# Graph convolution, layer 1: own rows added by VectorE, last two blocks gathered as plain rows, team pairs moved forward

## The chip, the cores and the metric

The kernel runs on one core of a Trainium2 chip. The metric is the device time of one execution in microseconds (us). The median of three runs of the kernel before is 2106.76 us, the lowest 2104.33, the highest 2110.44. Five engines run their own instruction streams in order, each waiting for the others by semaphores: TensorE (PE; its weight loads are listed as PEld), VectorE (DVE), ScalarE (ACT), GpSimd (POOL) and SyncE (SP), which issues most transfers. GpSimd issues the indirect transfers (gathers).

## The reference

Three graph convolution layers on 6250 nodes with 100,000 edges and one self loop for each node, widths 256, 512, 512, 256, then a residual and a layer norm:

```python
deg = jax.ops.segment_sum(jnp.ones_like(dst, dtype=x.dtype), dst, num_segments=n)
dinv = jnp.where(deg > 0, jax.lax.rsqrt(deg), 0.0)
norm_edge = dinv[src] * dinv[dst]
h = x
for W, b in ((W1, b1), (W2, b2), (W3, b3)):
    h = h @ W
    msg = h[src] * norm_edge[:, None]
    agg = jax.ops.segment_sum(msg, dst, num_segments=n)
    h = jax.nn.relu(agg + b)
x = _layernorm(x + h, axis=-1)
```

The edges come sorted by destination. A node's sum has the rows of its sources and, through the self loop, its own row.

## The kernel before

**Blocks and steps.** The nodes are 50 blocks of 125. Each layer (`layer`, with i = 0, 1, 2 for layers 1, 2, 3) forms the sums of a block in one of two ways. A *dense* block is the product of a matrix of edge counts with all rows of the table, 50 products (L1254); the counts are themselves made on the chip in layer 1 by `counts` (comparisons on VectorE, L784; products, L856) for 26 blocks and kept in DRAM. A *gathered* block fetches the rows of its edges, 16 gathers of 128 rows each (L1165), and multiplies each by a one-hot matrix (L1117, L1192). One step of the loop in `layer` (the variable `chunk`) issues one gather, the product of a gather some steps back (the *lag*), a few dense products, and one step of each piece of work under way (`go`, `go_fixed`). Where 10 blocks begin, one more gather fetches the rest of their edges. Layer 1 gathers blocks 22 to 49: 28 x 16 + 3 = 451 steps. Layer 2 gathers blocks 12 to 49, layer 3 blocks 29 to 49.

**Two halves.** TensorE multiplies in a rounded format. To keep precision a row is held as two halves, the rounded value and what is left, side by side. In layer 1 from block 26 on (`BOTH_FROM`) the gather fetches rows that are split already (table `both`, 512 elements, 2 KB) into one of 11 buffers named `halves`. Below block 26 it fetches plain rows (256 elements, 1 KB) which are multiplied unsplit. In layers 2 and 3 plain rows are fetched into a ring in `room` and split on the chip: ScalarE casts (L1219) and VectorE subtracts (L1222). `SPLIT` holds for each layer the lags of the cast, the subtraction and the product; layer 1 has (0, 0, 5).

**Own rows.** `parts` holds the split rows of all nodes on the chip. In layers 1 and 3 a gathered block's sum begins with a product of the identity with the block's own `parts` (L1177), into the same PSUM bank as the gathered products.

**After a block of layer 1** (`after1`): ScalarE scales the second half of the sum by `dinv` (L1284), VectorE scales the first and adds it (L1286), TensorE transposes (L1275) and multiplies by W1 (L1301), VectorE adds the bias (L1306), ScalarE applies the relu (L1309), and SP stores the result into layer 2's table (L72). Layer 2's first gather waits for the whole of that table.

**Stores for comparisons.** `counts` writes its comparisons into a rotating set of stores in `room`, two at first; when gathers into plain rows end in layer 1 (block 26), a third (`late_hot_room`), which lies where part of the ring of plain rows was, is added.

**Teams.** Layer 2's first 12 blocks are dense, but computed by `teams`: four groups of three blocks, three banks, 50 rows of blocks to go over; one call of its `next` issues one *pair*, that is, the two products (L964) of a block's counts with both halves of a row block, and now and then the load of the next two row blocks (SP, L74, three buffers), casts of counts (ScalarE, L916) and the split of the next row block (L924 on ScalarE, L926 on VectorE). The teams begin in layer 1 as soon as its 22 dense blocks are done, at one pair a step, go on while layer 1's last blocks drain, and run on in layer 2 at one pair a step; a whole pass is 600 pairs. Near their end (`returning`) layer 2 gives back four split buffers that lie in `parts`.

**The step between the layers.** At step 1 of layer 2 ScalarE and VectorE begin to split gathered rows, in order, each waiting for its gather; whatever the teams want of them after that is behind it. At step 5 SP is given the loads of W2 and W3.

Of the kernel before, what the change touches and what calls it, by code (L numbers as in the profile page):

```python
# [26 lines left out]
Q = 125  # L27
# [22 lines left out]
FEW = 22  # L50
BOTH_FROM = 26
BOTH_LAG = 5
SPLIT = ((0, 0, BOTH_LAG), (1, 2, 8), (3, 4, 9))
EXTRA = 4
TEAM = 3
TEAMS = 4
# [338 lines left out]
def sorted_path(ctx: ExitStack, tc: tile.TileContext, x, edges, starts, found, wts, biases, room, late, out):  # L395
# [367 lines left out]
    def counts(blocks, places, rush=0, at_once=False):  # L763

        def bank_for_pair():
            if at_once:
                return common.popleft() if len(common) > SPARE and len(full) < COUNTING else None
            if held.get("tr", 0) == 0:
                held["tr"] = 1
                return tr_bank  # L770

        def bank_back(bank):
            if at_once:
                common.append(bank)
            else:
                cooling.append(ticks + SOON)

        def compared(out, numbers):
            shape = list(out.shape)
            nc.vector.tensor_tensor(out, near_cols[:, :shape[2]].unsqueeze(1).to_broadcast(shape),  # L784
                                    numbers.unsqueeze(2).to_broadcast(shape), op=ALU.is_equal)

        hot = {}
        total = len(blocks) * GB
        ticks = 0
        bank, pair, full, whole = None, [], [], []  # L790

        def oldest_copied():
            if full:
                copied(full[0][0])
                return True

        if at_once:
            early_copy[0] = oldest_copied

        cooling = []  # L800

        def copied(now_on):
            while cooling and cooling[0] <= now_on:
                cooling.pop(0)
                free("tr")
            while whole and whole[0][0] <= now_on:
                _, n = whole.pop(0)
                place = places[n % len(places)]
                own = place[:, blocks[n], :]
                nc.vector.tensor_tensor(own, own, loops[:Q, :Q], op=ALU.add)  # L810
                by_rows(nc.sync, place.rearrange("p k v -> p (k v)"), kept[blocks[n]], store=True)
                if at_once:
                    there.append(now + 1)
            while full and full[0][0] <= now_on:
                _, counted_in, ms = full.pop(0)
                n, u = divmod(ms[0], GB)
                place = places[n % len(places)]
                nc.scalar.copy(place[:, :, u * G:(u + len(ms)) * G].rearrange("p k (t r) -> p t k r", r=G),  # L818
                               counted_in.rearrange("p (t v) -> p t v", t=2)[:Q, :len(ms), :NB * G]
                               .rearrange("p t (k r) -> p t k r", r=G))  # L820
                bank_back(counted_in)
                if u + len(ms) == GB:
                    whole.append((now_on + 1, n))

        for s in range(total + 4):
            if s < total and s % GB == 0:
                while (blocks[s // GB] + 1) * GB > seen * Q:
                    yield 1
            if s < total and s % WIDE == 0:
                t, w = divmod(blocks[s // GB] * GB + s % GB, Q)  # L830
                hot_stores.rotate(-1)
                hot_lo = hot_stores[-1][:, :WIDE * Q].rearrange("p (w v) -> p w v", v=Q)
                hot_key = hot_stores[-1][:, WIDE * Q:].rearrange("p (w v) -> p w v", v=G * NB)
                hot[s // WIDE] = hot_lo, hot_key
                compared(hot_lo, slots[:, t, 0, w:w + WIDE])
                compared(hot_key[:, :3], slots[:, t, 1, w:w + 3])
            if s < total and s % WIDE == 2:
                t, w = divmod(blocks[s // GB] * GB + s % GB + 1, Q)
                compared(hot[s // WIDE][1][:, 3:], slots[:, t, 1, w:w + WIDE - 3])
            copied(ticks)  # L840
            m = s - 4
            if 0 <= m:
                while at_once and finished < FEW and m // GB >= finished + len(places):
                    ticks += 1
                    yield 1
                    copied(ticks)
                while bank is None:
                    bank = bank_for_pair()
                    if bank is None and at_once and full and full[0][0] <= ticks + COPIED - 2:
                        copied(full[0][0])  # L850
                    elif bank is None:
                        ticks += 1
                        yield 1
                        copied(ticks)
                hot_lo, hot_key = [h[:, m % WIDE] for h in hot[m // WIDE]]
                nc.tensor.matmul(bank[:Q, len(pair) * 256:][:, :G * NB], lhsT=hot_lo, rhs=hot_key,  # L856
                                 start=True, stop=True)
                pair.append(m)
                if len(pair) == 2 or m % GB == GB - 1:
                    full.append((ticks + (COPIED if at_once else ALONE_COPIED), bank, pair))  # L860
                    bank, pair = None, []
            if s % 2 if s < rush else s % 2 or not rush:
                ticks += 1
                yield 1
        while full or whole or cooling:
            ticks += 1
            yield 1
            copied(ticks)
# [166 lines left out]
    def layer(i, width, gathered, dense, after, rows, first=0, spacing=1.0, extras=(), filler=None):  # L1035
# [97 lines left out]
        def of_both(c):  # L1133

            n, b, _ = items[c]
            return i == 0 and (n * GRP if b is None else b) >= BOTH_FROM

        def halved(c):

            return 0 <= c < total and items[c][1] is not None and i > 0  # L1140
        acc = None

        of_ten, to_split = {}, {}
        ten_halves = split.popleft() if i == 1 else None
# [2 lines left out]
        def gather(c):  # L1147
            nonlocal turn
            n, b, j = items[c]
            table = both_halves if of_both(c) else tables[i]  # L1150
            if (i, b, j) == (0, BOTH_FROM, BOTH_LAG + 1):
                hot_stores.appendleft(late_hot_room)
            if b is None:
                row, at = split.popleft() if of_both(c) else shared[n % 2], rest[:, n, 0:1]
                of_ten[n] = row
                if i == 1:
                    to_split[c + SPLIT[i][2] + 1] = n
            elif of_both(c):
                row, at = split.popleft(), src[:, b, j:j + 1]
                split_rows[c] = row  # L1160
            else:
                row, at = rows[turn % len(rows)], src[:, b, j:j + 1]
                (landed if i > 0 else split_rows)[c] = row
                turn += 1
            nc.gpsimd.indirect_dma_start(out=row, out_offset=None, in_=table,  # L1165
                                         in_offset=bass.IndirectOffsetOnAxis(ap=at, axis=0))

        def product(c):
            nonlocal acc
            n, b, j = items[c]  # L1170
            if b is None:
                return
            if j == 0:
                acc = sum_bank("acc", 2 if i == 1 else 3)
                if i != 1:

                    nc.tensor.matmul(acc[:Q], lhsT=ident_r[:Q, :Q], rhs=parts[:, b], start=True, stop=False)  # L1177
            if i == 1 and j == KF - LATE:
# [4 lines left out]
            for k, row in several:  # L1183
# [5 lines left out]
                    hot = hot.bitcast(F32)  # L1189
                size = min(row.shape[1], HID)  # L1190
                for c0 in range(0, row.shape[1], size):
                    nc.tensor.matmul(acc[:Q, :size], lhsT=hot, rhs=row[:, c0:c0 + size], start=(i == 1 and k == c0 == 0),  # L1192
                                     stop=(k == KF and c0 + size == row.shape[1]))
            halves = several[0][1]
            if i == 1 and halves in loaned:
# [10 lines left out]
        with tc.manual_schedule():  # L1206
            more_hots()
            to_sum = 0
            for chunk in range(total + (SHORT if i == 1 else lag)):
                now = chunk  # L1210
                if i == 1:
                    lag = SPLIT[i][2] if returning is None else max(SHORT, SPLIT[i][2] - (chunk - returning) // 2)
                if chunk < total:
                    gather(chunk)
                if halved(chunk - hi_lag):
                    halves = split_rows[chunk - hi_lag] = split.popleft()
                    if i == 1 and halves in loaned:
# [13 lines left out]
                    to_sum += 1  # L1231
                go(chunk)
                go_fixed(chunk)
                until = min(len(dense) * NB, begun + int((chunk + 1 - first) * NB / spacing))
                if i == 0:
                    until = min(until, done + 3)
# [43 lines left out]
    def after1(b, acc, bank):  # L1280
        got = []
        yield from take("zs", 2)
        zs = work.tile([Q, HID], F32, name="szs")
        nc.scalar.activation(zs[:, :C], acc[:Q, C:], AF.Copy, scale=dinv[:, b:b + 1])  # L1284
        yield 1
        nc.vector.scalar_tensor_tensor(zs[:, :C], acc[:Q, :C], dinv[:, b:b + 1], zs[:, :C], op0=ALU.mult, op1=ALU.add)  # L1286
        common.append(acc)
        yield SOON + 2
        turns = yield from one_of_common(0)
# [388 lines left out]
```

## Time and profile before

| | |
|---|---|
| median of three runs | 2106.76 us |
| the profiled execution's own time | 2105.52 us |
| its span, first to last instruction | 2103.8 us |
| mean granted TensorE clock | 0.981 |
| busy share: TensorE, VectorE, ScalarE, GpSimd | 92%, 73%, 64%, 68% |
| HBM traffic over the span | 236 GB/s |
| layer 1's last gather, layer 2's first | 709.65 us, 726.91 us |
| layer 3's first gather | 1652.79 us |

A row of a group reads: line, engine, operation, output <- input, shapes, count | busy us, mean ns of one | idle us of the engine just before, and what ended it. A row of a timeline reads: start, duration, engine, line, operation, output <- input, shapes, count [idle us before <- what ended it]. A row of windows reads: stretch, its length, then for each engine the busy us and the number of instructions, the granted TensorE clock, the busy share of the DMA engines (a sum over packets, which can pass 1) and GB/s. A row of DMA issues ends with the median us from issue to landing. A matmul's duration is that of one in a pipeline; the next can start earlier.

### The profile page before, as it was taken

The numbers are of one execution on the slowest core, as the hardware profiler recorded it, in microseconds if no ns is written. First come the engines' busy times: TensorE is split into PE (matmuls) and PEld (weight loads), VectorE is DVE, ScalarE is ACT, GpSimd is POOL, SyncE is SP. The second block draws the span as 40 slices with busy tenths as digits, with TensorE's granted clock in tenths as the row PEclk, the third lists the DMA queues.
The fourth block names the chain that finished last, engine by engine and source line by source line (L and its number), as shares of the span: only waits on it lengthen the run. The fifth ranks groups of instructions, "written<-read, shape, count | busy, mean of one in ns | idle before, by whom it ended". The sixth has DMA issues, their size and how long they took to land.

```text
span 2103.8 us, 30100 instructions
## 1 busy us (share of the span) xinstructions
PE 1943.4 (92%) x8711; PEld 1513.4 (72%) x8711; DVE 1527.7 (73%) x2877; ACT 1338.6 (64%) x2552; POOL 1435.4 (68%) x1442
## 2 busy tenths in 40 slices
PE   3499999999998689999999999999989899999997
PEld 2377777777774457788878777778777787887775
DVE  5877677777776288877787677777887377777777
ACT  1566777677775367767777666677766466555553
POOL 2466766676667477766776677667776477777775
PEclk9999999999999899999999999999999999999998
DMA  7887989999999999999999999889997366767674
GB/s 166 257 254 220 251 238 245 241 263 249 245 263 323 271 276 264 262 276 276 264 265 259 263 268 270 252 228 287 276 262 227 98 185 182 191 175 191 178 187 120
DMA packets 238728, 497.92 MB, mean 237 GB/s; under 512 B 43633, under 2 KB 86215, under 8 KB 238553
## 3 DMA queue, kind: packets, MB, share of 16 engines
q0 software_dynamic: 125184, 315.61, 54.6%
q1 hardware_dynamic: 97529, 168.45, 29.3%
q10 hardware_dynamic: 15840, 11.86, 2.2%
q8 instruction: 70, 1.15, 0.2%
q14 instruction: 105, 0.86, 0.1%
HBM read 428.29 MB, written 67.46 MB: 236 GB/s over the span
## 4 chain that ended last, share of the span: by engine, by line
PE 64%; DMA 17%; issue 7%; POOL 4%; DVE 4%; ACT 3%; ACTq 1%; SPq 0%; DVEq 0%; POOLq 0%
PE sacc L1192 12%; DMA room<-tab,ssrc 11%; PE mat_ps L1254 6%; PE smm L1254 6%; PE win_ps L1254 6%; PE win_ps L1364 5%; PE sacc L1254 5%; POOL room L1165 4%; PE win_ps L1384 3%; DMA halves<-both,ssrc 3%; PE str L1254 2%; PE mat_ps L964 2%; PE smm L964 2%; PE sacc L964 2%; PE sacc L1301 2%
## 5 line engine op out<-in xcount | busy, mean ns | idle before, releaser
L1165 POOL DMA_INDIRECT room<-tab,ssrc x1008 | 1039.2, 1031 | 386.9 <-issue 162.5
L1222 DVE TENSOR_TENSOR halves<-room,halves 128x512 fp32r<-128x512 f32 (+1 forms) x733 | 404.2, 566 | 230.1 <-ACT halves L1219 224.7
L1219 ACT CAST halves<-room 128x512 fp32r<-128x512 f32 (+1 forms) x733 | 367.7, 521 | 240.1 <-DMA room<-tab,ssrc 176.6
L1192 PE MATMUL sacc<-halves,shot 128*125 128x512 f32 x1375 | 481.4, 411 | 23.2 <-DMA halves<-both,ssrc 14.0
L1165 POOL DMA_INDIRECT halves<-both,ssrc x384 | 363.0, 945 | 158.5 <-issue 37.0
L1126 ACT CAST piece<-room 125x625 fp32r<-125x625 uint8 x416 | 294.3, 716 | 74.7 <-DVE halves L1222 22.7
L1192 PEld LDWEIGHTS sacc<-halves,shot 128*125 128x125 f32 x1375 | 255.3, 189 | 100.9 <-DMA halves<-both,ssrc 23.3
L784 DVE TENSOR_TENSOR room<-near_cols,slots 128x625 bf16<-128x625 f32 (+2 forms) x390 | 294.3, 803 | 36.7 <-PE sacc L856 15.6
L1117 DVE TENSOR_TENSOR shot<-near_cols,sdlo 128x500 fp32r<-128x500 f32 x371 | 248.3, 669 | 15.7 <-PE smm L1192 6.3
L1364 PE MATMUL win_ps<-room,w_sb 128*128 128x250 f32 (+1 forms) x832 | 191.0, 372 | 12.4 <-ACT room L1338 6.3
L1254 PE MATMUL mat_ps<-parts,piece 125*125 125x512 f32 x650 | 188.2, 406 | 0.3 <-ACT piece L1126 0.3
L1364 PEld LDWEIGHTS win_ps<-room,w_sb 128*128 128x128 f32 x832 | 154.4, 192 | 40.1 <-ACT room L1338 8.4
L1222 DVE TENSOR_TENSOR parts<-room,parts 128x512 fp32r<-128x512 f32 x211 | 143.7, 692 | 46.7 <-ACT parts L1219 41.2
L1254 PE MATMUL win_ps<-parts,piece 125*125 125x512 f32 x600 | 172.0, 408 | 5.0 <-ACT piece L1126 5.0
L1254 PE MATMUL smm<-parts,piece 125*125 125x512 f32 x605 | 173.0, 404 | 0.8 <-DVE piece L1126 0.6
L1219 ACT CAST parts<-room 128x512 fp32r<-128x512 f32 x211 | 128.7, 622 | 62.9 <-DMA room<-tab,ssrc 39.4
L926 DVE TENSOR_TENSOR parts<-parts 125x512 fp32r<-125x512 f32 x200 | 138.1, 691 | 35.2 <-ACT parts L924 34.8
L964 PE MATMUL sacc<-parts 125*125 125x512 f32 x400 | 140.4, 427 | 23.2 <-ACT parts L924 17.3
L1254 PE MATMUL sacc<-parts,piece 125*125 125x512 f32 x450 | 142.3, 423 | 2.5 <-ACT piece L1126 2.5
L818 ACT CAST room<-sacc 125x500 uint8<-125x500 f32 (+1 forms) x152 | 105.6, 703 | 60.8 <-PE sacc L856 59.2
L856 PEld LDWEIGHTS <-room 128*125 128x125 bf16 x650 | 88.9, 139 | 74.0 <-issue 26.6
L964 PE MATMUL mat_ps<-parts 125*125 125x512 f32 x400 | 137.1, 424 | 0.7 <-DVE st L1306 0.7
(308 smaller groups left out, 3139.4 us busy)
## 6 DMA issues: line engine op xcount, KB each, us to landing
parts<-tab SPq DMA_DIRECT2D x106, 448.0 KB
kept<-room SPq DMA_DIRECT2D x29, 683.6 KB
room<-kept SPq DMA_DIRECT2D x29, 683.6 KB
room<-tab,ssrc POOLq DMA_INDIRECT x1008, 5.5
tab<-st SPq DMA_DIRECT2D x62, 224.0 KB
both<-parts SPq DMA_DIRECT2D x10, 1120.0 KB
own_row<-tab SPq DMA_DIRECT2D x38, 224.0 KB
parts<-kept SPq DMA_DIRECT2D x60, 136.7 KB
```

The costliest lines, as they stand in the source:

```text
L784: nc.vector.tensor_tensor(out, near_cols[:, :shape[2]].unsqueeze(1).to_broadcast(shape), numbers.unsqueeze(2).to_broadcast(shape), op=ALU. ...
L818: nc.scalar.copy(place[:, :, u * G:(u + len(ms)) * G].rearrange("p k (t r) -> p t k r", r=G), counted_in.rearrange("p (t v) -> p t v", t=2 ...
L926: nc.vector.tensor_sub(to[:, HID:], row, to[:, :HID].bitcast(F32))
L964: nc.tensor.matmul(team_banks[n][:Q], lhsT=team_pieces[(g * CUTS + k // PIECE) % 2][n][:, k % PIECE, :], rhs=both_parts[u % 3][:, h * HID: ...
L1117: nc.vector.tensor_tensor(hot[:, :n], near_cols[:, :Q].unsqueeze(1).to_broadcast([P, n, Q]), dlo.rearrange("p b j -> p (b j)")[:, at:at + ...
L1126: convert(piece, made_or_read[:, c * PIECE:(c + 1) * PIECE, :])
L1165: nc.gpsimd.indirect_dma_start(out=row, out_offset=None, in_=table, in_offset=bass.IndirectOffsetOnAxis(ap=at, axis=0))
L1192: nc.tensor.matmul(acc[:Q, :size], lhsT=hot, rhs=row[:, c0:c0 + size], start=(i == 1 and k == c0 == 0), stop=(k == KF and c0 + size == row ...
L1219: nc.scalar.copy(halves[:, :width], landed[chunk - hi_lag])
L1222: nc.vector.tensor_sub(halves[:, width:], landed.pop(chunk - lo_lag), halves[:, :width].bitcast(F32))
L1254: nc.tensor.matmul(acc_d[:Q], lhsT=got[done // PIECE][:, k % PIECE, :], rhs=parts[:, k], start=(k == 0), stop=(k == NB - 1))
L1364: nc.tensor.matmul(h_ps[:, f, :], lhsT=w2_sb[:, k, (f2 + f) * P:(f2 + f + 1) * P], rhs=zt2[:, k, :wide], start=(k == 0), stop=(k == KH - 1))
```

## The change

- Own rows, layer 1, blocks 26 to 49: the identity product is not issued, and the first gathered product starts the bank. In `after1` VectorE adds `parts` to the whole sum (512 wide), ScalarE scales the second half in SBUF, VectorE scales and adds the first.
- Blocks 48 and 49 of layer 1 (`TAIL_FROM`) are gathered as plain rows into the ring in `room` and split on the chip, with lags 3 and 4. The lag of the product is 7 over the steps of block 48 (`TAIL_LAG`) and 5 elsewhere. The ring needs the third store's place: `counts` drops that store from its 22nd block on.
- One more team pair is issued at odd steps of layer 1 from the first gather of block 48 to the loop's end, and 12 (`FRONT`) at step 1 of layer 2 ahead of its first split.

```diff
+TAIL_FROM = 48
+TAIL_LAG = 7
+FRONT = 12
-SPLIT = ((0, 0, BOTH_LAG), (1, 2, 8), (3, 4, 9))
+SPLIT = ((3, 4, BOTH_LAG), (1, 2, 8), (3, 4, 9))
...
                 hot_stores.rotate(-1)
+                if at_once and s >= FEW * GB and hot_stores[-1] is late_hot_room:
+                    hot_stores.pop()
+                    hot_stores.rotate(-1)
...
-            return i == 0 and (n * GRP if b is None else b) >= BOTH_FROM
+            return i == 0 and (n * GRP >= BOTH_FROM if b is None else BOTH_FROM <= b < TAIL_FROM)
...
-            return 0 <= c < total and items[c][1] is not None and i > 0
-        acc = None
+            return 0 <= c < total and items[c][1] is not None and (i > 0 or items[c][1] >= TAIL_FROM)
+        acc = own_product = None
...
-                (landed if i > 0 else split_rows)[c] = row
+                assert i > 0 or b < TAIL_FROM or len(hot_stores) == 2
+                (landed if halved(c) else split_rows)[c] = row
...
-                if i != 1:
+                own_product = i == 2 or i == 0 and b < BOTH_FROM
+                if own_product:
...
-                    nc.tensor.matmul(acc[:Q, :size], lhsT=hot, rhs=row[:, c0:c0 + size], start=(i == 1 and k == c0 == 0),
+                    nc.tensor.matmul(acc[:Q, :size], lhsT=hot, rhs=row[:, c0:c0 + size], start=(not own_product and k == c0 == 0),
...
+                if i == 0:
+                    lag = TAIL_LAG if TAIL_FROM * KF <= chunk - total + NB * KF < (NB - 1) * KF else BOTH_LAG
                 if chunk < total:
                     gather(chunk)
+                if i == 1 and chunk == hi_lag:
+                    for _ in range(FRONT):
+                        next(team_work)
...
                 go_fixed(chunk)
+                if i == 0 and chunk % 2 and chunk >= total - (NB - TAIL_FROM) * KF:
+                    next(team_work)
...
-        nc.scalar.activation(zs[:, :C], acc[:Q, C:], AF.Copy, scale=dinv[:, b:b + 1])
-        yield 1
-        nc.vector.scalar_tensor_tensor(zs[:, :C], acc[:Q, :C], dinv[:, b:b + 1], zs[:, :C], op0=ALU.mult, op1=ALU.add)
+        if b < BOTH_FROM:
+            nc.scalar.activation(zs[:, :C], acc[:Q, C:], AF.Copy, scale=dinv[:, b:b + 1])
+            yield 1
+            nc.vector.scalar_tensor_tensor(zs[:, :C], acc[:Q, :C], dinv[:, b:b + 1], zs[:, :C], op0=ALU.mult, op1=ALU.add)
+        else:
+            nc.vector.tensor_tensor(zs, acc[:Q], parts[:, b].bitcast(F32), op=ALU.add)
+            nc.scalar.activation(zs[:, C:], zs[:, C:], AF.Copy, scale=dinv[:, b:b + 1])
+            yield 1
+            nc.vector.scalar_tensor_tensor(zs[:, :C], zs[:, :C], dinv[:, b:b + 1], zs[:, C:], op0=ALU.mult, op1=ALU.add)
         common.append(acc)
```

More of the change, by code (lines that the diff above doesn't have):

```diff
@@ L1168, in product @@
         def product(c):
-            nonlocal acc
+            nonlocal acc, own_product
             n, b, j = items[c]
```

## The prediction

> **What bounds the kernel now.** I read the busy times by window first, to see which engine each stage saturates; then the gather line in the same windows, to turn them into a pace; then the timelines around the step from layer 1 to layer 2.
>
> ```profile
> core 0: us, PE busy (x) PEld busy (x) DVE busy (x) ACT busy (x) POOL busy (x), PEclk, DMA share, GB/s
> 220.00:640.00 420.00, 418.63 (x1972) 309.53 (x1970) 311.89 (x524) 308.09 (x534) 292.36 (x311) 1.00 0.93 251
> 668.00:717.00 49.00, 40.10 (x133) 25.14 (x132) 16.53 (x27) 14.82 (x27) 30.12 (x31) 0.90 1.22 293
> 726.00:737.00 11.00, 0.61 (x3) 0.18 (x1) 0.72 (x2) 1.37 (x3) 7.65 (x9) 0.68 1.00 337
> 800.00:1540.00 740.00, 717.75 (x3251) 583.28 (x3250) 576.84 (x929) 517.95 (x962) 526.65 (x496) 1.00 0.95 264
> 1550.00:1610.00 60.00, 53.10 (x241) 43.16 (x239) 47.81 (x80) 40.33 (x79) 45.90 (x45) 0.97 0.88 254
> ```
>
> From 220 to 640 us (layer 1 while dense blocks are still multiplied) TensorE is never idle: an instruction less there is time less. From 668 to 717, the last two blocks, it is idle for 8.9 of 49 us and the granted clock is 0.90: here it waits for rows. From 726 to 737 it does almost nothing: the gap between the layers. In layer 2 it is busy for 97% while the team pairs run (800 to 1540) and 88% after them (1550 to 1610).
>
> The waits from 640 to 720 us (in total, times, longest) name what the last blocks lack, the landing of gathered rows:
>
> ```profile
> PEld sacc L1192 <- DMA halves<-both,ssrc: 23.3, 24, 1.7
> ```
>
> ```profile
> 666.47 0.94 POOL L1165 DMA_INDIRECT halves<-both,ssrc  x1 [0.30 <-issue]
> ...
> 709.65 1.17 POOL L1165 DMA_INDIRECT halves<-both,ssrc  x1 [0.60 <-PE sacc L1192]
> 726.91 0.96 POOL L1165 DMA_INDIRECT room<-tab,rest  x1 [16.10 <-DMA tab<-st]
> 728.18 0.95 POOL L1165 DMA_INDIRECT room<-tab,ssrc  x1 [0.30 <-issue]
> ```
>
> The last 32 gathers start from 666.47 to 709.65: 43.18 / 31 = 1.39 us each, where GpSimd alone could start one each 0.94 + 0.30 = 1.24 us. After the last, GpSimd waits 16.1 us for layer 1's table to be stored, and layer 2 begins.
>
> **Own rows.** The change takes the identity product (L1177) from 24 blocks, 26 to 49.
>
> ```profile
> 185.00:640.00 455.00, 8.36 (x21) 3.90 (x21) 1.00 0.93 249
> 640.00:720.00 80.00, 1.50 (x3) 0.70 (x3) 0.87 1.19 305
> ```
>
> ```profile
> 592.09 0.39 PE L1177 MATMUL str<-parts,ident_r 125*125 125x512 f32 x1
> 592.32 0.40 PE L1192 MATMUL str<-halves,shot 128*125 128x512 f32 x1
> ```
>
> These windows hold that line alone: 21 of the 24 lie in the saturated stretch. The next product starts 0.23 us later, and that step, not the 0.39 us of one pipelined product, is its price: 21 x 0.23 = **4.8 us less**. The other three lie where TensorE waits anyway. In exchange VectorE adds a 125x512 block out of PSUM, the form of L1306, and then scales and sums as before:
>
> ```profile
> L1306 DVE TENSOR_TENSOR st<-sacc,room 125x512 f32<-125x512 f32 x20 | 13.7, 685 | 9.5 <-PE sacc L1301 9.5
> ...
> L1284 ACT ACTIVATE szs<-sacc,sdinv 125x256 f32<-125x256 f32 x12 | 5.7, 479 | 1.5 <-PE sacc L1254 1.4
> ```
>
> 0.69 us of VectorE for each block lies beside TensorE's work, because VectorE is busy for 311.89 of 420 us; were that cover gone it would cost 21 x 0.69 = 14.5 us. ScalarE's scaling now reads SBUF; no row has that form, so I keep the 0.48 us (half and twice that are the bounds: 0.2 less or 0.5 more, on the last block alone). The add waits in VectorE's queue for the block's last product, and the comparisons for the counts stand behind it; VectorE waited there already, one step later, for ScalarE. For the last block nothing covers it: the chain from last product to stored table becomes 0.7 us longer: **+0.7**.
>
> The third store for comparisons is dropped for the last 100 count steps (20 groups of 5). With two stores, at 120 to 190 us, the first comparison of a group waited 15.5 us in 14 groups; with three, at 594 to 640, 1.8 us in 13:
>
> ```profile
> L784 DVE TENSOR_TENSOR room<-near_cols,slots 128x625 bf16<-128x625 f32 x14 | 11.3, 811 | 15.5 <-PE smm L856 6.6 <-PE sacc L856 4.4 <-PE mat_ps L856 3.9
> ```
>
> ```profile
> L784 DVE TENSOR_TENSOR room<-near_cols,slots 128x625 bf16<-128x625 f32 x13 | 10.5, 808 | 1.8 <-PE sacc L856 1.1 <-PE win_ps L856 0.4 <-PE str L856 0.2
> ```
>
> ```profile
> 594.00:640.00 46.00, 44.63 (x219) 32.63 (x217) 38.33 (x60) 34.14 (x60) 32.30 (x35) 1.00 1.02 261
> ```
>
> A group takes 46 / 13 = 3.5 us of time and 38.33 / 13 = 2.9 us of VectorE. I cost the drop at nothing: that wait ends when TensorE has passed the group two before, which leaves a group's time for 2.9 us of work. If its 1.1 us (15.5 / 14) simply added to 2.9, it would be 0.5 us for 13 groups, 6.5 us at most.
>
> **Last two blocks.** 32 gathers now fetch 1 KB rows instead of 2 KB; ScalarE casts and VectorE subtracts 128x256 for each, as in layer 3:
>
> ```profile
> L1222 DVE TENSOR_TENSOR halves<-room,halves 128x256 fp32r<-128x256 f32 x230 | 93.3, 419 | 75.5 <-ACT halves L1219 75.3
> ...
> L1219 ACT CAST halves<-room 128x256 fp32r<-128x256 f32 x228 | 86.7, 402 | 64.2 <-DMA room<-tab,ssrc 59.3 <-DVE halves L1222 3.0 <-DVE szs L1417 1.5
> ```
>
> Both are hidden, since ScalarE is busy 14.82 and VectorE 16.53 of the 49 us, and 32 x 0.4 = 13 us is added to each. GpSimd's work is not less, so the pace can fall to 1.24 at best: 31 x 0.15 = 4.7 us; at worst it stays. I take **3 us less**, nearer to the floor, since plain rows have a ring of 8 beside the 11 split buffers. From issue to landing:
>
> ```profile
> halves<-both,ssrc POOLq DMA_INDIRECT x31, 8.9
> ```
>
> ```profile
> halves<-both,ssrc POOLq DMA_INDIRECT x147, 4.8
> ```
>
> ```profile
> room<-tab,ssrc POOLq DMA_INDIRECT x232, 3.4
> ```
>
> 8.9 is the median in the tail now (at 293 GB/s), 4.8 that of the same gathers from 400 to 600 us, 3.4 that of layer 3's 1 KB rows. The last gather's product now starts 716.75 - 709.65 = 7.1 us after the issue (rows below). With 4.8, the two operations (0.82) and about 0.3 for the hops it is 5.9: **1.2 us less**; 3.4 would give 2.6 less, 8.9 would give 2.9 more. I take 4.8, because 32 x 128 KB = 4.2 MB leave a stretch of 14 MB, which brings its load near that row's.
>
> **Team pairs.** Layer 1 counts 451 steps and 5 of lag; odd steps from 419 to 455 are 19, and 12 pairs more stand ahead of the first split: 31.
>
> ```profile
> 716.75 0.73 PE L1192 MATMUL sacc<-halves,shot 128*125 128x512 f32 x2 [1.30 <-DMA halves<-both,ssrc]
> ...
> 725.34 0.63 PE L964 MATMUL mat_ps<-parts 125*125 125x512 f32 x2
> 725.80 0.63 PE L964 MATMUL smm<-parts 125*125 125x512 f32 x2
> ```
>
> A pair steps by 0.46 us. 19 x 0.46 = 8.7 us fits into the 8.9 idle us of the tail, just; cover gone, it costs up to 8.7. The 12 are 5.5 us in this gap:
>
> ```profile
> 736.82 0.79 PE L964 MATMUL sacc<-parts 125*125 125x512 f32 x1 [10.39 <-ACT parts L924]
> ```
>
> ```profile
> 735.63 0.62 ACT L1219 CAST halves<-room 128x512 fp32r<-128x512 f32 x1 [10.80 <-DMA room<-tab,rest]
> ```
>
> What they need (casts of rows and counts) now stands on ScalarE behind the first split, which waits 10.8 us for the first gather; put ahead, nothing holds it. They start nothing for layer 2 sooner, so the gap's end stays. Four units of rows also issue two loads (0.5 MB each) on SP, ahead of the weights:
>
> ```profile
> 724.60 0.82 SPq L74 DMA_DIRECT2D parts<-tab  x2
> 725.51 0.39 SPq L1550 DMA_DIRECT2D w_sb<-in_L_gnn_W  x1
> 726.00 0.45 SPq L1553 DMA_DIRECT2D w<-in_L_gnn_W  x1
> ```
>
> 1 MB at the window's 337 GB/s is 3 us of lateness for the first gathers at worst; but SP reaches the weights (1.5 MB) later, as a load waits until its buffer is read, so the gathers could also land up to 4 us sooner (7.4 us now, from 728.18 to the cast at 735.63, against 3.4). I take 0. The Trainium skill, "DMA: Bandwidth & Descriptors", section "Queues, rings and completion order", says that each DMA engine takes turns between the queues it has work for, a packet at a time. By that the two loads would slow the first gathers, not block them: the sum would be some 1.5 us higher, an estimate from that page. The trace agrees that they share: those gathers land later than layer 3's.
>
> The gain comes where these pairs are missing later. This line's windows count gathers:
>
> ```profile
> 800.00:1540.00 740.00, 526.65 (x496) 1.00 0.95 264
> 1550.00:1610.00 60.00, 45.90 (x45) 0.97 0.88 254
> ```
>
> A step of layer 2 takes 740 / 496 = 1.49 us with a pair and 60 / 45 = 1.33 without. The teams end 31 steps sooner, and these run without: 31 x 0.16 = **4.9 us less**. Lower bound 0; upper bound 31 x 0.46 = 14.3, if TensorE alone set the pace. I take the measured paces.
>
> The profile also shows a granted clock of 0.68 in the gap. The Trainium skill, "TensorE: Matmul & The Clock Gate", Part 1, puts the array at half clock after an idle window of about 3.4 us. The idle left after the 12 pairs is some 4.9 us, still longer, so by the rule the drop may stay; nothing for it is in my sum.
>
> **Sum.** -4.8 + 0.7 - 3 - 1.2 - 4.9 = -13.2, against the profiled execution's 2105.5 us (span 2103.8 and 1.7 around it): 2092.3. The median of the runs stands 1.2 higher: **2093 us**.
>
> **Rivals.**
> - *Pairs are worth their full time in layer 2.* For: TensorE busy for 97% there. Against: 88% without pairs, and 1.33 is near GpSimd's 1.24. 9.4 us less than the forecast: 2084.
> - *VectorE takes the time over.* The adds, and comparisons with one store less, hold up the counts' products. For: 2.9 of 3.5 us busy from 594 to 640. Against: 26% free over the whole stretch. Price up to 14.5, which takes the gain: 2107.
> - *Slower: landings stay long in the tail.* A lap of the ring of 8 plain rows is 0.95 for the issue, the landing, 0.82 for the two operations and about 1.2 for waits in order. From a landing of 8 x 1.39 - 3.0 = 8.1 us on, the tail is slower than now; at 8.9 a gather takes 11.9 / 8 = 1.48 us. ScalarE then waits for each landing, and the casts of the 19 pairs stand behind it, while the pairs stand ahead of the products on TensorE. 32 x 0.09 = 2.9, 2.9 on the last landing, up to 8.7 for the pairs and 3 for the first gathers, with -4.8, +0.7 and -4.9 as above: +8.5, so 2115. For: 8.9 us now, and a gather still has 128 rows. Against: 4.8 us at 249 GB/s.
>
> **Chances.** Forecast 0.60, full time 0.10, VectorE 0.17, long landings 0.13. A measurement of this kernel tells about 0.3% (6.3 us) from no change. Below 2100.4 fall nearly all of the first two and a little of the third: faster 0.68; slower (above 2113) 0.12; the same 0.20. The range of 8 in 10 leaves out half of the slow case and the far end of the full-time case: 2081 to 2109. The forecast's own range is 2085 to 2101.
>
> **What would show it.** L1177 gone for 24 blocks, and TensorE still saturated up to about 635 us: own rows right; idle time there ended by L784 or L1286: VectorE took it over. The last 32 gathers at 1.24 to 1.30 us, landing in about 5: the tail right; 1.5 or more and 8 us: long landings. TensorE busy for some 5 us more ahead of the first split, which still ends a wait for its gather: the 12 pairs right. Team pairs in layer 2 ending some 31 steps earlier, with the steps after them at 1.33: the last term right; at more than 1.4 it is nothing. A later layer would show no change of its own. The forecast is wrong if layer 1's table is not complete some 8 us sooner.

## The result: 0.3% less, and the profile after

The changed kernel takes 2099.93 us (median of 20 runs, 2089.86 to 2107.37), the kernel before 2104.93 in 20 runs beside it: a ratio of 0.9968 with a 95% interval of 0.9955 to 0.9981, that is 6.7 us less (4.0 to 9.5). The prediction was 2093 us, from a sum of -13.2. A later comparison gave 0.9978 (0.9959 to 0.9996). The profiled execution after has a span of 2097.8 us.

The same stretches as before, where the change has moved a stage by its new times (the columns are those explained above):

```profile
220.00:640.00 420.00, 417.12 (x1963) 308.09 (x1962) 323.49 (x543) 310.67 (x538) 294.35 (x312) 1.00 0.94 252
668.00:717.00 49.00, 45.44 (x175) 30.86 (x174) 34.35 (x70) 33.76 (x74) 32.04 (x32) 1.00 1.03 260
726.00:737.00 11.00, 8.61 (x33) 5.56 (x31) 2.48 (x4) 3.60 (x6) 6.94 (x7) 1.00 0.97 264
800.00:1499.00 699.00, 682.59 (x3085) 554.04 (x3083) 546.77 (x883) 492.01 (x916) 497.11 (x472) 1.00 0.95 265
1500.00:1610.00 110.00, 95.77 (x424) 77.42 (x424) 82.46 (x138) 70.24 (x136) 82.22 (x83) 0.97 0.85 246
```

TensorE is still saturated up to 640 us, is busy for 45.4 of the tail's 49 us instead of 40.1, and does 8.6 us of work in the gap between the layers instead of 0.6. VectorE has 12 us more to do up to 640, beside TensorE. The teams end at 1499 us instead of 1541. All of this is as the prediction drew it; the time is not, and one of its signs is missing: layer 2's first gather, which waits for layer 1's table, starts at 728.23 us (722.44 in the profile of change_again, the same kernel) and not some 8 us sooner than 726.91.

Clean stages are read best from one gather to another, by their starts on GpSimd. First the kernel before, gathers 64 and 384 of layer 1 (320 steps apart, some 20 blocks), then the changed kernel, the same two and the last 32 (numbers 419 and 450):

```profile
179.78 0.96 POOL L1165 DMA_INDIRECT room<-tab,ssrc  x1 [0.39 <-PE win_ps L1192]
...
620.95 0.94 POOL L1165 DMA_INDIRECT halves<-both,ssrc  x1 [0.30 <-PE sacc L856]
```

```profile
183.42 0.95 POOL L1172 DMA_INDIRECT room<-tab,ssrc  x1 [0.39 <-PE win_ps L1200]
...
619.78 0.94 POOL L1172 DMA_INDIRECT halves<-both,ssrc  x1 [0.31 <-PE sacc L862]
...
667.80 1.35 POOL L1172 DMA_INDIRECT room<-tab,ssrc  x1 [0.30 <-DMA halves<-both,ssrc]
...
708.55 0.95 POOL L1172 DMA_INDIRECT room<-tab,ssrc  x1 [0.31 <-issue]
```

620.95 - 179.78 = 441.17 us before, 619.78 - 183.42 = 436.36 after: 4.8 less. The last 32 gathers go at 40.75 / 31 = 1.31 us instead of 1.39. The table has these distances for every profile of a chip like the first one ("drain": from layer 1's last gather to its last product; layers 2 and 3 count from their own first gather, layer 3 to the end; the kernels are explained below):

| profile | #64 to #384 | #384 to layer 2 | of it last 32 | drain | layer 2 | layer 3 |
|---|---|---|---|---|---|---|
| before | 441.2 | 106.0 | 43.2 | 7.4 | 925.9 | 451.1 |
| change | 436.4 | 108.5 | 40.8 | 9.0 | 918.2 | 451.3 |
| change_again | 436.4 | 104.7 | 40.6 | 8.0 | 922.8 | 452.3 |
| own_only | 436.4 | 108.7 | 41.1 | 9.2 | 925.2 | 450.0 |
| tail_only | 441.1 | 107.3 | 40.6 | 8.7 | 925.5 | 452.1 |
| own_tail_again | 436.4 | 105.2 | 40.0 | 8.3 | 918.5 | 450.2 |
| own_three | 436.4 | 103.5 | 40.1 | 6.9 | 922.9 | 452.3 |
| pairs_only | 441.2 | 116.6 | 47.5 | 11.6 | 922.0 | 453.5 |
| no_tail | 436.4 | 114.7 | 49.0 | 9.6 | 929.6 | 454.4 |
| only_19_again | 441.2 | 118.4 | 46.1 | 12.5 | 933.3 | 450.6 |

The first column repeats to 0.05 us; layer 2 scatters by some 10 us between single executions, so only groups of profiles can be compared there. Each row is one execution: that of only_19_again was the longest of its run, 13 us above the median, and that of own_tail_again the shortest, 11 us below it.

### The profile page after: what moved, and what is told of

Read it like the earlier page. It is cut to its first block, busy times and chain, and to the rows that moved or that the text cites. A ratio compares the mean times of both kernels' runs of the same rounds, so it can differ in the third digit from the quotient of the medians.

```text
span 2097.8 us, 30169 instructions
## 1 busy us (share of the span) xinstructions
PE 1944.3 (93%) x8687; PEld 1513.0 (72%) x8687; DVE 1555.1 (74%) x2933; ACT 1351.9 (64%) x2584; POOL 1432.8 (68%) x1442
## 4 chain that ended last, share of the span: by engine, by line
PE 61%; DMA 17%; issue 8%; POOL 6%; DVE 4%; ACT 2%; ACTq 1%; SPq 0%; POOLq 0%; DVEq 0%
DMA room<-tab,ssrc 13%; PE sacc L1200 11%; PE mat_ps L1269 7%; PE smm L1269 6%; POOL room L1172 6%; PE win_ps L1269 6%; PE win_ps L1385 5%; PE sacc L1269 5%; PE str L1269 2%; PE win_ps L1405 2%; PE sacc L1322 2%; PE mat_ps L970 2%; PE sacc L970 2%; PE smm L970 2%; PE win_ps L1200 1%
## 5 line engine op out<-in xcount | busy, mean ns | idle before, releaser
L1172 POOL DMA_INDIRECT room<-tab,ssrc x1040 | 1069.2, 1028 | 398.4 <-issue 168.5
L1235 DVE TENSOR_TENSOR halves<-room,halves 128x512 fp32r<-128x512 f32 (+1 forms) x778 | 427.1, 562 | 242.3 <-ACT halves L1232 233.4
L1232 ACT CAST halves<-room 128x512 fp32r<-128x512 f32 (+1 forms) x778 | 388.9, 517 | 229.9 <-DMA room<-tab,ssrc 175.3
L1200 PE MATMUL sacc<-halves,shot 128*125 128x512 f32 x1384 | 479.4, 411 | 15.4 <-DVE shot L1123 6.6
L1172 POOL DMA_INDIRECT halves<-both,ssrc x352 | 331.0, 940 | 143.6 <-issue 36.8
L787 DVE TENSOR_TENSOR room<-near_cols,slots 128x625 bf16<-128x625 f32 (+2 forms) x390 | 294.2, 801 | 44.9 <-PE sacc L862 21.3
L1235 DVE TENSOR_TENSOR parts<-room,parts 128x512 fp32r<-128x512 f32 x198 | 134.2, 689 | 46.8 <-ACT parts L1232 43.6
L1232 ACT CAST parts<-room 128x512 fp32r<-128x512 f32 x198 | 120.1, 622 | 52.5 <-DMA room<-tab,ssrc 37.1
```

What stands on the lines that cost most here:

```text
L1232: nc.scalar.copy(halves[:, :width], landed[chunk - hi_lag])
L1235: nc.vector.tensor_sub(halves[:, width:], landed.pop(chunk - lo_lag), halves[:, :width].bitcast(F32))
```

## The experiments

**The four parts, on one chip** (29 runs of the kernel before, median 2106.72). Each kernel is the change with some parts taken back.

*own_only*: own rows by VectorE and nothing else.

```diff
-TAIL_FROM = 48
+TAIL_FROM = 50
-FRONT = 12
+FRONT = 0
-                if i == 0 and chunk % 2 and chunk >= total - (NB - TAIL_FROM) * KF:
+                if False and chunk >= total - (NB - TAIL_FROM) * KF:
```

(and the third store kept)

> Own rows by VectorE for blocks 26 to 49 and nothing else of the change (no plain rows in the last two blocks, third store kept, no team pair moved). Theory A (each term of the prediction holds, the rest is scatter): 21 products x 0.23 us less and the last block's chain 0.7 longer, -4.1 us (ratio 0.998). Theory B (the last two blocks as plain rows give nothing or cost time, the other terms hold): the same -4.1 us. Rival (VectorE takes the time over): 0 or slower, with TensorE idle before 640 us ended by VectorE.

Measured: 2100.51 us, ratio 0.9962 (0.9943 to 0.998), 8 us less (4.2 to 12.0). The stretch from #64 to #384 has its 4.8 us, the size that was worked out; where the rest would lie is not shown. One part alone brings all that the whole change brings.

*pairs_only*: the 19 and the 12 pairs moved, identity products and 2 KB rows as before.

```diff
-TAIL_FROM = 48
+TAIL_FROM = 50
-                if i == 0 and chunk % 2 and chunk >= total - (NB - TAIL_FROM) * KF:
+                if i == 0 and chunk % 2 and chunk >= total - 2 * KF:
-                own_product = i == 2 or i == 0 and b < BOTH_FROM
+                own_product = i != 1
-        if b < BOTH_FROM:
+        if b < NB:
```

> The 19 pairs of the last two blocks and the 12 ahead of layer 2's first split, nothing else of the change. Theories A and B: -4.9 us (ratio 0.9977), team pairs ending about 31 steps earlier in layer 2. Rival (pairs are worth their full time): -14 us. Rival (the pairs only move work, layer 2's pace is set by GpSimd and landings): 0, the last pair earlier but layer 3's first gather not.

Measured: 2117.28 us, ratio 1.0056 (1.0035 to 1.0076): 11.8 us **more** instead of less. The last 32 gathers take 47.5 us instead of 43.2, the drain 11.6 instead of 7.4.

*tail_only*: plain rows in blocks 48 and 49 and the third store dropped; `own_product = i != 1` as in pairs_only, no pair moved.

> The last two blocks as plain rows with lags 3, 4 and 7 or 5, and the third store dropped; identity products kept, no team pair moved. Theory A: -4.2 us (ratio 0.998). Theory B: 0 to +4 us, the last product of layer 1 some 9 us after the last gather's issue instead of 7.

Measured: 2106.42 us, ratio 0.9991 (0.9971 to 1.001). In its profile the last 32 gathers gain 2.6 us and the drain loses 1.2; of the whole nothing is left that could be told from zero.

*no_tail*: own rows and all pairs, but 2 KB rows in the last two blocks (`TAIL_FROM = 50`, pairs from `total - 2 * KF` on).

> The whole change without its last two blocks as plain rows (and with the third store kept): own rows, 19 + 12 pairs. Theory A: -9.0 us, 4 us slower than the changed kernel. Theory B: -9 to -12 us, faster than the changed kernel (measured ratio 0.9968, -6.7 us).

Measured: 2112.9 us, ratio 1.0033 (1.0013 to 1.0052), 7 us more, although the own rows have their 4.8 us in it. Without plain rows the pairs cost more than the own rows bring, and with them (the change) they don't: plain rows and pairs act together. TensorE has the same products to do in both, so their time alone is not what costs.

**Which pairs, and what without them.** The next four ran on a chip where the kernel before takes 2329.52 us (35 runs), 11% longer; the last section has what is different there. The theories' letters are this group's own.

*own_tail*: `FRONT = 0` and no pair in the tail, else as the change.

> Own rows by VectorE and plain rows in the last two blocks, but no team pair is moved (neither the 19 of the tail nor the 12 ahead of layer 2's first split). Theory A (the moved pairs cost time, also beside plain rows): the own rows give their 8 us and the plain rows nothing, so 8 to 10 us less than before, 1 to 4 us less than the whole change. Theory B (beside plain rows the pairs fit into idle time and give back 5 us in layer 2): only some 2 us less than before, as the whole change loses the layer 2 gain; the first gather of layer 2 starts at the same distance from gather 384 as with the whole change (108 to 109 us) under B, and 1 to 3 us sooner under A.

*own_tail_19*: `FRONT = 0`, else as the change.

> Own rows, plain rows and the 19 pairs of the tail, without the 12 ahead of layer 2's first split. Theory A (the cost of the moved pairs arises in the tail): within 2 us of the whole change, 6 to 7 us less than before. Theory C (the cost arises from the 12, whose loads stand ahead of layer 2's first gathers): 9 to 12 us less than before, and the time from layer 2's first gather to its first product falls from 14.9 to 13.7 us.

*only_19*: pairs_only with `FRONT = 0`.

> The kernel before with only the 19 pairs of the tail moved (identity products and split rows stay). Theory A: their loads and products disturb a tail that already waits for its rows, so 8 to 12 us more than before; the last 32 gathers take 46 to 48 us instead of 43.2. Theory C: the 19 fit into the idle time of the tail, within 2 us of before, last 32 gathers 43 to 44 us.

*only_front*: pairs_only without the pairs of the tail.

> The kernel before with only the 12 pairs ahead of layer 2's first split. Theory A: within 2 us of before, layer 2 some 2 us shorter (12 steps x 0.16). Theory C: 8 to 10 us more than before; layer 2's first product comes 15 us or more behind its first gather instead of 13.7, and the steps after it are slower too.

Measured: own_tail 2333.09 us, ratio 1.0017 (0.9999 to 1.0035); own_tail_19 2334.9, 1.0031 (1.0004 to 1.0059); only_19 2335.84, 1.002 (0.9995 to 1.0044); only_front 2330.07, 0.9991 (0.9964 to 1.0017). On this chip not even own rows with plain rows are faster: TensorE is busy for 396.8 of the 420 us from 220 to 640 in own_tail, so it isn't saturated, and the distance from #64 to #384 is 484.3 with own rows against 485.8 and 487.1 without (only_front, only_19). These runs can't be set beside the first four; that the 12 cost nothing that can be told is all that they say of theory C.

*own_tail_again* and *change_again*: the kernels own_tail and the whole change beside each other, on a chip like the first.

> The same kernel as own_tail (own rows and plain rows, no pair moved), beside the whole change on one chip, since the chip of the last four runs takes 11% longer for the kernel before. On a chip like the first (before at 2105 us): theory A (the moved pairs cost time, also beside plain rows) 8 to 10 us less than before and 1 to 4 less than the whole change; theory B (beside plain rows the pairs pay) 2 us less than before and 4 to 5 more than the whole change; theory D (beside plain rows the pairs are worth nothing either way, they cost in the tail what they save in layer 2) within 2 us of the whole change. On a chip like the last (before at 2330 us): again +2 to +6 us, as TensorE is not saturated there and the identity products hide.

> The whole change once more. On a chip like the first: 6 to 7 us less than before under every theory. On a chip like the last: if the gain is the 21 identity products off a saturated TensorE, it is not there: 0 to 7 us more than before, as own_tail_19 without the 12 was 0.3% slower.

Measured beside 23 runs of the kernel before (2104.9): own_tail_again 2098.59 us, ratio 0.9966 (0.9954 to 0.9979); change_again 2100.15, 0.9978 (0.9959 to 0.9996), a little less gain than expected. They are 1.6 us apart with overlapping intervals: theory D, beside plain rows the moved pairs are worth nothing either way that could be told. B is out; a cost of 1 to 4 us (A) isn't excluded.

*only_19_again*: only_19 on a chip like the first.

> The kernel before with only the 19 pairs of the tail. If their loads (0.5 MB each) in a tail that waits for rows are the cost of moving pairs, this run carries nearly all of the 12 us that 19 and 12 together cost: 8 to 12 us more than before on a chip where before takes 2105 us, the last 32 gathers 46 to 48 us instead of 43.2, layer 2's first gather 8 to 11 us later. If the cost is the 12 ahead of layer 2's split, within 3 us of before.

Measured: 2113.53 us against 2105.3, ratio 1.0037 (1.0022 to 1.0051), 7.8 us more; the last 32 gathers 46.1 us, layer 2's first gather 118.4 us behind #384 instead of 106.0. The 19 carry most of what the 31 cost. What they do is seen in the DMA view, from the first of the last 32 gathers to layer 2's first one. The rows: packets in all; per queue packets, MB and share; issues with their count and the median time to landing. The kernel before (666 to 727 us):

```profile
DMA packets 9309, 16.65 MB, mean 273 GB/s; under 512 B 1158, under 2 KB 1908, under 8 KB 9306
...
q1 hardware_dynamic: 4109, 7.16, 49.9%
...
parts<-tab SPq DMA_DIRECT2D x8, 448.0 KB
...
halves<-both,ssrc POOLq DMA_INDIRECT x33, 8.9
```

only_19_again (671 to 741 us):

```profile
DMA packets 10397, 18.31 MB, mean 262 GB/s; under 512 B 1302, under 2 KB 2427, under 8 KB 10392
...
q1 hardware_dynamic: 5252, 8.90, 55.8%
...
parts<-tab SPq DMA_DIRECT2D x12, 448.0 KB
...
halves<-both,ssrc POOLq DMA_INDIRECT x32, 10.9
```

Pairs moved into the tail bring their rows with them: 12 loads instead of 8, and 8.90 - 7.16 = 1.74 MB more on SP's queue, 6.4 us at 273 GB/s, in a stage that waits for its rows. The gathers land after 10.9 us instead of 8.9. Now the same stretch with plain rows, own_tail_again (657 to 717 us) and change_again (663 to 722 us):

```profile
q1 hardware_dynamic: 4179, 7.30, 43.6%
...
room<-tab,ssrc POOLq DMA_INDIRECT x32, 5.1
```

```profile
q1 hardware_dynamic: 5499, 9.34, 58.0%
...
room<-tab,ssrc POOLq DMA_INDIRECT x32, 6.8
```

The pairs lengthen the landing here too, by 1.7 us, but from 5.1, and the ring of plain rows still covers it: the last 32 gathers take 40.6 us with the pairs and 40.0 without.

*own_three*: own_tail, and VectorE adds the own rows in layer 3 as well.

```diff
-                own_product = i == 2 or i == 0 and b < BOTH_FROM
+                own_product = i == 2 and b == NB - 1 or i == 0 and b < BOTH_FROM
...
+            nc.vector.tensor_tensor(whole, acc[:Q], parts[:, b].bitcast(F32), op=ALU.add)
```

> own_tail_again with one thing more: in layer 3, too, VectorE adds the own rows, for all gathered blocks but the last (20 identity products less). If the price of 0.23 us for each product off a saturated TensorE carries over, 3.2 us (the 14 in the stretch where TensorE is busy for 299.8 of 300 us) to 4.6 us (all 20) less than own_tail_again, so 10 to 12 us less than before on a chip where before takes 2105 us; layer 3 from its first gather to the end 450 to 446 us. Rival: the 20 adds of 0.69 us on VectorE (busy for 74% there, and each holding up a one-hot or a subtraction) take that back, layer 3 stays at 450 us or grows.

Measured: 2101.87 us against 2105.3, ratio 0.9983 (0.9964 to 1.0002): no gain over own_tail_again that could be told, and not the 10 to 12 us less that were expected; layer 3 takes 452.3 us instead of 450.2. The reason stands in the windows of 1700 to 2000 us, first own_tail_again, then own_three:

```profile
1700.00:2000.00 300.00, 299.83 (x1291) 239.55 (x1290) 221.73 (x594) 172.78 (x403) 229.31 (x233) 1.00 0.68 184
```

```profile
1700.00:2000.00 300.00, 297.86 (x1267) 234.81 (x1267) 229.81 (x601) 171.88 (x404) 229.60 (x232) 1.00 0.69 183
```

TensorE is busy for 299.8 of 300 us, which reads like a bound. But GpSimd issues 233 gathers, and each has 0.30 us ahead of it in the timelines: 229.31 + 233 x 0.30 = 299.2 us. No gap before a gather is longer than 0.32 us in that stretch: GpSimd is full as well. With 24 matmuls less there (14 of them the identity products) TensorE gets 2 us of idle time and GpSimd issues no gather more. In layer 1's stretch the same sum is 292.36 + 311 x 0.30 = 385.7 of 420 us: there GpSimd has room, and the identity products were time.

## Why the prediction was half right

**Own rows, 4.8 us less: right.** 441.2 to 436.4 in every pair of profiles. That stretch holds 20 of the products, so one is worth 0.24 us; that 20 x 0.24 and the predicted 21 x 0.23 agree to the tenth is luck. The price of a saturated TensorE's instruction is the step to the next one, not its duration (0.39). VectorE's cover held, with the two new forms close to what was taken:

```profile
L1305 ACT ACTIVATE szs<-szs,sdinv 125x256 f32<-125x256 f32 x20 | 10.2, 510 | 1.1 <-DVE szs L1304 1.1
...
L1304 DVE TENSOR_TENSOR szs<-sacc,parts 125x512 f32<-125x512 f32 x6 | 4.1, 687 | 2.2 <-PE sacc L1200 2.2
```

The add takes 0.687 us (0.69 taken), the scaling 0.510 instead of 0.479. The rival in which VectorE takes the time over fell. The 0.7 us for the last block can't be seen: from the last product to layer 2's first gather it is 9.8 us before, and 10.7 to 12.4 in the others, with own rows or without (11.6 in tail_only, 11.5 in pairs_only).

**Last two blocks, 3 us less: right (2.4 to 3.1). Last landing, 1.2 us less: not seen.** The drain is 8.0 to 9.0 us with the change instead of 7.4. Without moved pairs it is 7.4 and 9.2 us with 2 KB rows (before, own_only) and 8.7, 8.3 and 6.9 with plain rows (tail_only, own_tail_again, own_three): between single executions it scatters by 2 us, and neither a gain nor a loss can be told. From own_tail_again, the last gather and the cast of its row:

```profile
697.10 1.22 POOL L1172 DMA_INDIRECT room<-tab,ssrc  x1 [0.30 <-DVE shot L1123]
...
703.90 0.40 ACT L1232 CAST halves<-room 128x256 fp32r<-128x256 f32 x1 [2.31 <-DMA room<-tab,ssrc]
```

ScalarE waits for the landing until 703.90 - 697.10 = 6.8 us after the issue, where 4.8 was taken, the median of an uncrowded stretch; the cast and the subtraction follow. The third store, dropped at no cost in the prediction, shows none: from gather 384 to 419 it is 45.2 to 48.0 us without it (five profiles) and 44.9 to 48.1 with it (five). The wait that the prediction feared is there all the same: from 594 to 640 us the first comparison of a group waits 8.8 us in 12 groups after the change, 1.8 in 13 before, and VectorE's room covers it.

**Pairs in the tail at nothing: right for the whole change, for a reason that the prediction hadn't.** It set 8.7 us of products against 8.9 idle us of TensorE. What the pairs needed room on was the DMA engines, whose share stood in the row that it quoted: 1.22. Their rows found room because the plain rows had freed it: over the last 32 gathers the share is 1.27 and 1.31 with 2 KB rows (before, own_only), 0.93 with plain rows (own_tail_again) and 1.08 after the change. With 2 KB rows the engines moved 305 and 314 GB/s without the pairs and 301 to 308 with them; beside plain rows 240 to 245 became 270 to 278. Without that room the pairs cost 10.6 and 12.4 us by layer 2's first gather (pairs_only and only_19_again against before) and 6.0 (no_tail against own_only). No run moved loads without products or products without loads, so that it is the loads is argued from these rates and the landings. The rival of long landings named the right mechanism, but gave it to the plain rows.

**Twelve pairs ahead of layer 2's split at nothing: wrong, by about 1 us at the first product and more behind it.** From layer 2's first gather to its first product it is 13.7 to 14.6 us in the five profiles without moved pairs (mean 14.2) and 14.9 to 15.4 in the four with all of them (mean 15.1). The changed kernel's ScalarE there:

```profile
731.20 0.62 ACT L930 CAST parts<-parts 125x512 fp32r<-125x512 f32 x1 [4.17 <-DMA parts<-tab]
...
737.43 0.62 ACT L1232 CAST halves<-room 128x512 fp32r<-128x512 f32 x1 [3.25 <-DMA room<-tab,ssrc]
```

The pairs' own rows land late (ScalarE waits 4.17 us for them), and the first split still ends a wait for its gather, as predicted, 737.43 - 728.23 = 9.2 us after layer 2's first gather instead of 735.63 - 726.91 = 8.7. The sentence on the Trainium skill, "DMA: Bandwidth & Descriptors", section "Queues, rings and completion order" (an engine takes turns between its queues), had put 1.5 us on this: for the first product the size agrees, slowed and not blocked. That the loads of the 12 are the cause is not shown, since only_19_again has 16.0 us there without them. The larger loss comes behind the first product and is told with layer 2.

**Layer 2, 4.9 us less: this step failed.** The five profiles without moved pairs have 925.9, 925.2, 925.5, 918.5 and 922.9 us there, mean 923.6; the four with all 31 have 918.2, 922.8, 922.0 and 929.6, mean 923.2. The gain is 0.4 us with a standard error of 2.7 from the scatter, so that these profiles alone make 4.9 unlikely and no more; the runs side by side say the same, own_tail_again being 1.6 us below the whole change. The teams do end 31 steps sooner (92 pairs instead of 61 stand ahead of layer 2's first product). The first error lies in the price of a step: 1.49 - 1.33 us was taken for the pair, from windows that differ in more than the pair. The kernel before once more, by the products of layer 3's counts (L856) and by gathers:

```profile
800.00:1404.00 604.00, 18.50 (x68) 9.25 (x69) 0.99 0.95 262
1452.00:1541.00 89.00, 0.00 (x0) 0.00 (x0) 1.00 0.97 269
```

```profile
800.00:1404.00 604.00, 424.85 (x401) 0.99 0.95 262
1452.00:1541.00 89.00, 68.20 (x64) 1.00 0.97 269
1541.00:1610.00 69.00, 52.76 (x52) 0.95 0.91 260
```

Up to 1404 us a step takes 604 / 401 = 1.51 us and has a pair and the counts' work; from 1452 to 1541 the counts are gone, the pairs are not, and it takes 89 / 64 = 1.39; after that, without pairs, 69 / 52 = 1.33. Steps lose their pair at the end of the teams, so their price is 0.06 and not 0.16: 31 x 0.06 = 1.9 us. From gather 974 to 1004, the steps that lose their pair, the five profiles take 41.3 us on average and the four 40.4. GpSimd is full there in both cases: 68.20 + 64 x 0.30 = 87.4 of 89 us, 52.76 + 52 x 0.30 = 68.4 of 69 (a gather itself takes 1.07 and 1.01 us on average, the shortest 0.94; why is not shown). So a step gains little when TensorE has less to do. The rival in which the pairs are worth their full time falls with it.

The second error is at the start of the layer. Its gather 640 starts here, in the kernel before and in change_again:

```profile
998.57 0.94 POOL L1165 DMA_INDIRECT room<-tab,ssrc  x1 [0.30 <-issue]
```

```profile
1001.70 0.94 POOL L1172 DMA_INDIRECT room<-tab,ssrc  x1 [0.30 <-DVE halves L1235]
```

That is 271.7 and 279.3 us behind the layer's first gather. The five profiles without moved pairs have 269.4 to 274.5 there, the four with all 31 have 278.7 to 282.9: 8.2 us more on average, and from there to layer 3's first gather 8.6 less. The moved pairs do save time later, and the start of the layer takes it back. The waits that grew, from the first gather to gather 600 (in total, times, longest), first before, then in change_again:

```profile
POOL room L1165 <- DVE halves L1222: 12.6, 22, 2.4
...
DVE parts L926 <- ACT parts L924: 3.4, 4, 2.2
```

```profile
POOL room L1172 <- DVE halves L1235: 18.4, 22, 3.2
...
DVE parts L932 <- ACT parts L930: 17.4, 7, 4.6
```

VectorE's splits of the teams' rows wait for their casts on ScalarE, what stands behind them in VectorE's queue waits too, and GpSimd waits longer for the splits of gathered rows that give its buffers back. That this causes the loss is argued from these rows alone. With the 19 pairs alone it is 274.1 us to gather 640 (only_19_again), which points to the 12 or to all 31 together. The slower chip does not settle it: 294.8 without moved pairs (own_tail), 296.1 with the 12 (only_front), 295.1 and 299.9 with the 19 (only_19, own_tail_19).

**The sum.** With 0.4 us in place of layer 2's 4.9 (the later first product is in it) and nothing for the last landing, the prediction's -13.2 becomes -7.5; measured were -6.7 (-9.5 to -4.0) and in the later comparison -4.6 (-8.6 to -0.8). Own rows alone, and own rows with plain rows, give 8 and 7.2 us: the pairs can be left out. Which of the three versions is the fastest these intervals don't tell. The time lies in the forecast's own range (2085 to 2101 us) by 1 us, and that is in part luck, since two of the four terms that were to bring it did not. Of the signs that were named, the teams did end 31 steps sooner and the steps behind them did take 1.33 us: they show where the pairs went, not what that was worth.

## What to carry to other kernels

An idle engine is room for moved work only if that work's data also find room: read the DMA share of the stage before the idle time of the engine. The price of an instruction taken from a stage comes from a window of that stage which differs in nothing else, and a busy share of 97 to 100% does not name the bound: add up each engine's issue gaps too (here 0.30 us ahead of every gather) before one is chosen. And work that is gone at the end of a stage can have been paid for at its start: compare the times of the same gather along the whole stage.

## What the runs showed of the hardware beyond that

**Chips differ.** One chip took 2329.52 us for the kernel that takes 2105 on the others, with the same instructions. The transfers were no slower: the shares of SP's and GpSimd's transfers times the span are nearly the same. The kernel own_tail on the first kind of chip (own_tail_again's page, span 2085.6 us), then on the slower one (2331.1 us), with the first row of the chain of waits:

```profile
q0 software_dynamic: 122112, 311.41, 53.4%
q1 hardware_dynamic: 97529, 168.45, 29.1%
...
PE 62%; DMA 15%; issue 7%; DVE 7%; POOL 4%; ACT 3%; ACTq 1%; SPq 1%; DVEq 0%; POOLq 0%
```

```profile
q0 software_dynamic: 122112, 311.41, 48.2%
q1 hardware_dynamic: 97529, 168.45, 26.0%
...
PE 36%; issue 12%; POOL 5%; DVE 5%; ACT 3%; another core or an unknown queue 2%; DMA 1%; ACTq 0%; DVEq 0%; POOLq 0%; SPq 0%
```

53.4% of 2085.6 and 48.2% of 2331.1 us are 1114 and 1124. In the chain the time grows in which engines wait for nothing that the profile shows ("issue", 7% and 12%; "unknown queue"), but the parts of the second chain make only 65% of the span, so where the rest went is not shown. The longest such wait from 1900 to 2000 us is 7.3 us on VectorE. What it is was not tried. Layer 3 is hit most: 537.8 us instead of 450.

**The clock after a short gap.** After the 12 pairs TensorE idles from 736.4 to 740.8 us, 4.46 us instead of 10.39. The changed kernel's windows around it, by the pairs' line:

```profile
726.00:737.00 11.00, 8.61 (x33) 5.56 (x31) 1.00 0.97 264
736.50:741.00 4.50, 0.17 (x1) 0.17 (x1) 0.77 1.03 384
741.00:746.00 5.00, 3.68 (x8) 2.15 (x8) 0.53 1.05 340
```

The clock is 1.00 while the pairs run and 0.53 when work begins again, so filling the gap in part did not save the warm clock. The rule of the Trainium skill, "TensorE: Matmul & The Clock Gate", Part 1, which puts the array at half clock after some 3.4 us of idling, agrees with these rows.
